# Causal maxima in tiles of 32 tokens by four heads, instead of 128 tokens of one head

## The chip, the cores and the metric

The kernel runs on one core of a Trainium2 chip. The metric is the device time of one execution in microseconds. Before the change it is 818.26 us, the median of 3 runs (817.12 to 818.61).

## The reference, cut to what matters

The program is one transformer layer on 8 sequences (batches) of 256 tokens with 256 features: attention, then a mixture of experts. The change is in the attention alone. There are 32 query heads of width 8, and 8 key heads; each key head serves four query heads.

```python
q = (x @ Wq).reshape(b, T, N_HEADS, hd).transpose(0, 2, 1, 3)
k = (x @ Wk).reshape(b, T, N_KV_HEADS, hd).transpose(0, 2, 1, 3)
...
q = _apply_rope(q, cos, sin)
k = _apply_rope(k, cos, sin)
qg = q.reshape(b, N_KV_HEADS, N_GROUPS, T, hd)
scores = jnp.einsum('bkgtd,bksd->bkgts', qg, k) / jnp.sqrt(jnp.asarray(hd, x.dtype))
causal = jnp.tril(jnp.ones((T, T), dtype=bool))
scores = jnp.where(causal[None, None, None, :, :], scores, jnp.asarray(-jnp.inf, x.dtype))
attn = jax.nn.softmax(scores, axis=-1)
ctx = jnp.einsum('bkgts,bksd->bkgtd', attn, v)
```

Here `T` is 256, `hd` is 8, there are 8 key heads and 4 query heads ("groups") to each. A softmax subtracts from each row of scores its maximum over the keys that the row may see, which are those up to its own token.

## The kernel before

**Two passes over the scores.** The attention of a batch computes its scores twice. The first pass (`maxima`, L461) has tokens on the partitions: TensorE makes scores in PSUM, adds a mask of -1e30 above the diagonal with a second matmul, and VectorE takes the maximum over the keys, with its sign turned (L486). The negated maxima are split into a high and a low part (`split_shift`, L494), turned by TensorE so that heads come to the partitions (`shiftT`, L501), and written by DMAs as extra rows 96 to 101 into the tile of queries. The second pass (`weights_of`, L521) has keys on the partitions; its matmul runs over 102 rows, so the maximum is subtracted inside the matmul. ScalarE takes the exponential (L532), GpSimd clears what lies above the diagonal (L534), and `values` (L545) multiplies by the values.

**Operands.** `qAs` holds the queries turned, as [row, (chunk, group), token]: a chunk is three key heads (the last has two) that share the 96 rows, 32 rows for each head. `ksts` holds the keys, [row, key head, token], with zeros in the rows of the other heads, so that one matmul of a query tile of 96 rows against several key heads gives the scores of each head apart. There are three buffers of each, used by batch modulo 3. `queriesT` (L436) turns the queries on TensorE and copies them by ScalarE into `qAs` (L448), one copy for each chunk and each half of the tokens.

**Tiles of the first pass.** A step has 128 tokens of one query head of a group on the partitions, and two or three key heads times all keys up to the end of the 128 tokens as columns. For the first half of the tokens that is 128 keys, for the second half 256. `maxima_of` (L450) cuts this into steps of at most 512 columns, which is one PSUM tile `sc`. Each matmul of scores (L472) is followed by a matmul of the mask (L479), whose stationary operand is a 128x128 identity in bf16 (`ident_b`), and whose moving operand is the 128x128 triangle `mask`, repeated for each key head. For a batch that makes 26 steps, 32 matmuls of scores and 32 of the mask.

**Order.** All engines run an order that is written out: `at(when, step, ...)` puts each step on a timeline in units of batches, and the steps are issued in the order of `when` (L1197). The maxima of batch b start at b - 0.98, one every 0.032; between them lie the exponentials and values of batch b - 1, the projections of batch b + 1, and, from 1.5 on, the matmuls of the shared experts (`shared_gate_up`, `shared_down`), which fill TensorE. [...]The PSUM tiles of scores, of the second pass and of the experts come from one pool of five buffers (`ps_mm`).

**After the attention** come the blocks of routed experts, which TensorE runs one after another from some 545 us on; the change touches nothing there.

Of the kernel before, what the change touches and what calls it, by code (L numbers as in the profile page):

```python
# [10 lines left out]
F32 = mybir.dt.float32  # L11
F32R = mybir.dt.float32r
BF16 = mybir.dt.bfloat16
I32 = mybir.dt.int32
AF = mybir.ActivationFunctionType
ALU = mybir.AluOpType
AX = mybir.AxisListType
PSUM = bass.MemoryType.PSUM

P = 128  # L20
# [4 lines left out]
SHIFT = 96  # L25
# [5 lines left out]
def attn_moe_kernel(  # L31
# [47 lines left out]
    nc = tc.nc  # L79
    B, T, D = x.shape  # L80
# [11 lines left out]
    G = 4  # L92
    NKV = NH // G
    NK = NKV * HD
    NC = NKV // G
    J = 3
    NS = -(-NKV // J)
    KR = SHIFT + 2 * J
    QSCALE = HD**-0.5
    FT = 4  # L100
    NTOK = NT * P
# [11 lines left out]
    small = ctx.enter_context(tc.tile_pool(name="small", bufs=4))  # L113
    shared_pool = ctx.enter_context(tc.tile_pool(name="shared", bufs=1))
    ps_mm = ctx.enter_context(tc.tile_pool(name="ps_mm", bufs=5, space=PSUM))
# [3 lines left out]
    aconst = early.enter_context(tc.tile_pool(name="aconst", bufs=1))  # L119
# [12 lines left out]
    ident = const.tile([P, P], F32, name="ident")  # L132
# [8 lines left out]
    for w, lo, n in ((wq, 0, D), (wk, D, NK), (wv, D + NK, NK)):  # L141
        nc.scalar.dma_start(
            out=wqkv[:, :, lo : lo + n], in_=w.rearrange("(k p) n -> p k n", p=P)
# [3 lines left out]
    for b in range(1, B):  # L147
# [6 lines left out]
    nc.scalar.dma_start(out=wr_sb, in_=wr)  # L154


    mask = aconst.tile([P, P], BF16, name="mask")
    nc.gpsimd.memset(mask, 0.0)
    nc.gpsimd.affine_select(
        out=mask,  # L160
        in_=mask,
        pattern=[[-1, P]],
        compare_op=ALU.is_ge,
        fill=NEG,
        base=0,
        channel_multiplier=1,
    )
    ident_b = aconst.tile([P, P], BF16, name="ident_b")
    nc.vector.tensor_copy(ident_b, ident)
    ident_r = aconst.tile([P, P], F32R, name="ident_r")  # L170
    nc.vector.tensor_copy(ident_r, ident)

# [4 lines left out]
    for sign, base in ((1, 0), (-1, 1)):  # L177
        nc.gpsimd.affine_select(
            out=place1[SHIFT:P],
            in_=place1[SHIFT:P],  # L180
            pattern=[[-2 * sign, J], [0, 1]],
# [5 lines left out]
    qAs, ksts, v_aug = {}, {}, {}  # L187

    def clear_operands(i):
        qAs[i] = aconst.tile([P, NS * G, T], F32R, name=f"qA_{i}")  # L190
        engine = nc.gpsimd if i > 0 else nc.vector
        engine.memset(qAs[i][:, (NS - 1) * G :, :].bitcast(F32), 0.0)
        t = ksts[i] = aconst.tile([P, NKV, T], F32R, name=f"kst_{i}")
        engine.memset(t[0:SHIFT].bitcast(F32), 0.0)

# [103 lines left out]
    def at(when, step, *args):  # L299
        timeline.append((when, len(timeline), step, args))  # L300
# [100 lines left out]
    def heads_in(c):  # L401
        return min(J, NKV - c * J)
# [33 lines left out]
    def queriesT(b, tt, c):  # L436
        qs = held["qs", b, tt][1]
        n = heads_in(c) * HB
        pt = ps_tp.tile([P, G, P], F32, tag="tp", name=f"pqT{b}_{tt}_{c}")
        for g in range(G):  # L440
            nc.tensor.matmul(
                pt[0:n, g, :],
                lhsT=qs[:, c * G + g, 0:n],
                rhs=ident_r,
                start=True,
                stop=True,
            )
        nc.scalar.copy(qAs[b % 3][0:n, ts(c, G), ts(tt, P)], pt[0:n])  # L448

    def maxima_of(b, tt):  # L450

        width = (tt + 1) * P
        for c in range(NS):
            per = min(512 // width, heads_in(c))
            for k0 in range(0, heads_in(c), per):
                nk = min(per, heads_in(c) - k0)
                ng = 512 // (nk * width)
                for g0 in range(0, G, ng):
                    yield c, c * J + k0, nk, g0, ng

    def maxima(b, tt, c, k0, nk, g0, ng):  # L461

        qA, kst = qAs[b % 3], ksts[b % 3]
        if ("nmx", b, tt) not in held:
            held["nmx", b, tt] = small.tile(
                [P, NKV, G], F32, tag="nmx", name=f"nmx{b}_{tt}", bufs=2
            )
        nmx = held["nmx", b, tt]
        width = (tt + 1) * P
        sc = ps_mm.tile([P, ng, nk, width], F32, tag="mm", name="sc")  # L470
        for g in range(ng):
            nc.tensor.matmul(  # L472
                sc[:, g, :, :],
                lhsT=qA[0:SHIFT, c * G + g0 + g, ts(tt, P)],
                rhs=kst[0:SHIFT, k0 : k0 + nk, 0:width],
                start=True,
                stop=False,
            )
            nc.tensor.matmul(  # L479
                sc[:, g, :, width - P :],  # L480
                lhsT=ident_b,
                rhs=mask.unsqueeze(1).to_broadcast([P, nk, P]),
                start=False,
                stop=True,
            )
        nc.vector.tensor_reduce(  # L486
            nmx[:, k0 : k0 + nk, g0 : g0 + ng].rearrange("p k g -> p g k"),
            sc,
            AX.X,
            ALU.max,  # L490
            negate=True,
        )

    def split_shift(b, tt):  # L494
        nmx = held.pop(("nmx", b, tt))
        nhl = small.tile([P, NKV, 2, G], F32R, tag="nhl", name=f"nhl{b}_{tt}", bufs=2)
        nc.vector.tensor_copy(nhl[:, :, 1, :], nmx)
        nc.vector.tensor_tensor(nhl[:, :, 0, :], nmx, nhl[:, :, 1, :], ALU.subtract)
        held["nhl", b, tt] = nhl

    def shiftT(b, tt):  # L501
        nhl = held.pop(("nhl", b, tt))
        pm = ps_tp.tile([2 * NH, P], F32, tag="tp", name=f"pm{b}_{tt}")
        nc.tensor.matmul(
            pm,
            lhsT=nhl.rearrange("p k a g -> p (k a g)"),
            rhs=ident_r,
            start=True,
            stop=True,
        )  # L510
        nm = work.tile([2 * NH, P], F32R, tag="nm", name=f"nm{b}_{tt}")
        nc.vector.tensor_copy(nm, pm)
        for c in range(NS):
            n = 2 * heads_in(c)
            lo = c * J * 2 * G
            nc.sync.dma_start(
                out=qAs[b % 3][SHIFT : SHIFT + n, ts(c, G), ts(tt, P)].bitcast(F32),
                in_=nm[lo : lo + n * G, :].bitcast(F32),
            )

    def weights_of(b, kv, s, t):  # L521

        sc = ps_mm.tile([P, G, P], F32, tag="mm", name="scT")
        nc.tensor.matmul(  # L524
            sc,
            lhsT=ksts[b % 3][0:KR, kv, ts(s, P)],
            rhs=qAs[b % 3][0:KR, ts(kv // J, G), ts(t, P)],
            start=True,
            stop=True,
        )  # L530
        e = work.tile([P, G, P], F32, tag="ex", name="ex", bufs=EX)
        nc.scalar.activation(e, sc, AF.Exp, scale=QSCALE)  # L532
        if s == t:
            nc.gpsimd.affine_select(  # L534
                out=e,
                in_=e,
                pattern=[[0, G], [1, P]],
                compare_op=ALU.is_ge,
                fill=0.0,
                base=0,  # L540
                channel_multiplier=-1,
            )
        held["ex", b, kv, s, t] = e
# [437 lines left out]
    def turning(xg, b):  # L981


        n = xg.shape[1]
        xgT = ffn.tile([P, KC, n * P], F32, tag=f"xgT{n}", name=f"xgT{b}")
        of = xg.rearrange("p t (k d) -> p k t d", k=KC)
        to = xgT.rearrange("p k (t q) -> p k t q", q=P)

        def step(i):
            for j in range(P // SQ):  # L990
                nc.vector.transpose(  # L991
                    to[ts(j, SQ), :, :, ts(i, SQ)], of[ts(i, SQ), :, :, ts(j, SQ)]
                )

        return xgT, [partial(step, i) for i in range(P // SQ)]
# [66 lines left out]
    for i, a in enumerate((-2.2, -0.93, 0.03)):  # L1062
        at(a, clear_operands, i)
        at((-1.7, a, a)[i], set_ones, i)
        at((-1.97, -0.96, 0.02)[i], clear_values, i)
# [13 lines left out]
    for b in range(B):  # L1079
# [14 lines left out]
        when = b - 0.98  # L1094
        for tt in range(TT):
            for m in maxima_of(b, tt):
                at(when, maxima, b, tt, *m)
                when += 0.032
            at(when + 0.001, split_shift, b, tt)
            at(when + 0.07, shiftT, b, tt)  # L1100
        last = b == B - 1
        parts_of = [(c, t) for c in range(NC) for t in range(TT)]
        when, unit = b, 0.98 / (NC * 3 * G)
        if b == 0:
            parts_of.sort(key=lambda part: part[1])
            when, unit = -0.4, 0.04
        for c, t in parts_of:
            if b == 0 and t > 0:
                when = max(when, 0)
            for s in range(t + 1):  # L1110
                for j in range(G):
                    at(when, weights_of, b, c * G + j, s, t)
                    when += unit
                at(when + 0.05, values, b, c, s, t)
            a = when + (0.1 if last else 0.12)
            at(a, softmaxed, b, c, t)
            if c == NC - 1:
                at(a + 0.05, contextT, b, t)
                at(a + 0.09, projected, b, t)
# [84 lines left out]
    for b in range(NFULL):  # L1204
# [12 lines left out]
        xg, now, steps = held.pop(("xg", b + 1)), xgT, ()  # L1217
        if b + 1 < NFULL:
            xgT, steps = turning(xg, b + 1)
# [122 lines left out]
```

## Time and profile before

| What | Value |
|---|---|
| median of 3 runs | 818.26 us |
| the profiled execution: its own time | 817.86 us |
| the profiled execution: span from first to last instruction | 815.8 us |
| mean granted TensorE clock | 0.97 |
| ScalarE busy | 251.3 us (31%) |
| GpSimd busy | 344.0 us (42%) |
| exponential of the second pass, L532, on ScalarE | 192 times 597 ns |
| copy of the queries, L448, on ScalarE | 48 times, 576 to 580 ns |
| clearing above the diagonal, L534, on GpSimd | 128 times 639 ns |
| matmul of the second pass, L524 | 192 times, 512 columns |
| DMA of the maxima into `qAs`, L514 | 32 of 12 KB and 16 of 8 KB |

The profile names engines PE (TensorE matmuls), PEld (TensorE loads of the stationary operand, which may run beside a matmul), DVE (VectorE), ACT (ScalarE), POOL (GpSimd) and SP. Matmuls are pipelined, so the duration of one is longer than the distance from its start to the start of the next; in a stream it is the distance of the starts that says what a matmul costs.

### The profile page before, as it was taken

The page shows a single profiled execution, that of the slowest core. Times are in us where ns is not written, and L with a number is a line of the kernel's source. Part 1 is how long each engine was busy: PE and PEld are TensorE (multiplying, and loading weights), DVE is VectorE, ACT ScalarE, POOL GpSimd, SP SyncE. Part 2 cuts the span into 40 slices and gives each one's busy share as a digit, 9 for nine tenths or more (in the row PEclk, how much of TensorE's full clock was granted, in tenths as well). Part 3 has the DMA queues.
Part 4 walks back from the last instruction along what each step waited for, and adds up shares of the span by engine and source line. Part 5 has one row for each costly group of instructions (what it writes and reads, how often), then busy time and mean ns, then how long its engine had stood idle before and what let it go on. Part 6 is the DMA issues. An engine that isn't in the chain of part 4 may idle for free. (4 is left out here: it accounts for less than half of the span.)

```text
span 815.8 us, 11856 instructions
## 1 busy us (share of the span) xinstructions
PE 761.7 (93%) x3977; PEld 579.3 (71%) x3977; DVE 492.2 (60%) x1412; ACT 251.3 (31%) x552; POOL 344.0 (42%) x620
## 2 busy tenths in 40 slices
PE   5989899999999999999999998799999999999992
PEld 3544467767776776776766657688888888888991
DVE  5756577667668568568666635547655555742226
ACT  2455344334334334333333431121111111111214
POOL 4567456426436436436324441416223434343323
PEclk8799899999999999999999998899999999999997
DMA  5033300000000000000000002365465665758544
GB/s 155 3 88 90 89 16 16 8 22 15 7 23 14 2 29 14 3 29 14 2 29 2 14 14 90 139 226 169 129 206 168 192 218 157 233 149 271 170 81 155
DMA packets 31011, 70.42 MB, mean 86 GB/s; under 512 B 8560, under 2 KB 25456, under 8 KB 28256
## 3 DMA queue, kind: packets, MB, share of 16 engines
q1 hardware_dynamic: 19504, 54.23, 19.2%
q0 software_dynamic: 8128, 9.77, 6.4%
q10 hardware_dynamic: 3312, 5.60, 2.4%
q8 instruction: 34, 0.56, 0.3%
q14 instruction: 33, 0.27, 0.1%
HBM read 55.16 MB, written 11.80 MB: 82 GB/s over the span
## 5 line engine op out<-in xcount | busy, mean ns | idle before, releaser
L780 PE MATMUL gu<-xgT,w 128*128 128x256 f32 (+1 forms) x840 | 163.9, 354 | 1.0 <-ACT xgT L978 0.7
L780 PEld LDWEIGHTS gu<-xgT,w 128*128 128x128 f32 x840 | 144.5, 190 | 18.1 <-ACT xgT L978 1.0
L532 ACT ACTIVATE ex<-scT 128x512 f32<-128x512 f32 x192 | 113.6, 597 | 137.4 <-PE scT L524 124.9
L780 PE MATMUL gu<-x2T,ws_sb 128*128 128x256 f32 x640 | 152.9, 385 | 0.1
L486 DVE TENSOR_REDUCE nmx<-sc 128x2 f32<-128x512 f32 (+2 forms) x208 | 129.3, 643 | 26.4 <-PE sc L479 26.1
L780 PEld LDWEIGHTS gu<-x2T,ws_sb 128*128 128x128 f32 x640 | 119.8, 193 | 21.3 <-ACT ex L532 3.8
L534 POOL TENSOR_SCALAR_AFFINE_SELECT ex<-ex 128x512 f32<-128x512 f32 x128 | 81.0, 639 | 114.3 <-ACT ex L532 114.1
L1014 POOL DMA_INDIRECT sums<-yb,of x37 | 58.5, 1582 | 109.2 <-DVE yb L1013 71.1
L472 PE MATMUL sc<-kst,qA 96*128 96x512 f32 (+2 forms) x256 | 101.3, 426 | 0.8 <-issue 0.5
L524 PE MATMUL scT<-qA,kst 102*128 102x512 f32 x192 | 97.5, 516 | 1.8 <-DMA qA<-nm 1.8
L1003 ACT ACTIVATE sg<-gu 128x256 f32<-128x256 f32 (+1 forms) x105 | 37.6, 358 | 191.1 <-PE gu L780 154.2
L991 DVE STREAM_TRANSPOSE xgT<-xg 32x128 f32<-32x128 f32 x240 | 72.6, 302 | 29.4 <-DMA xg<-rows,of 20.6
L793 PE MATMUL po<-w,act 128*128 128x256 f32 x370 | 83.1, 379 | 0.0
L793 PE MATMUL po<-ws_sb,sact 128*128 128x256 f32 x320 | 74.7, 391 | 4.6 <-DVE sact L816 4.6
L793 PEld LDWEIGHTS po<-w,act 128*128 128x128 f32 x370 | 69.8, 190 | 9.3
L793 PEld LDWEIGHTS po<-ws_sb,sact 128*128 128x128 f32 x320 | 61.6, 196 | 18.3 <-DVE sact L816 5.0
L479 PE MATMUL sc<-mask,ident_b 128*128 128x256 bf16 (+2 forms) x256 | 74.3, 293 | 0.0
L1004 DVE TENSOR_TENSOR act<-sg,gu 128x256 f32<-128x256 f32 (+1 forms) x105 | 38.8, 388 | 56.8 <-ACT sg L1003 56.2
L815 DVE SCALAR_TENSOR_TENSOR th<-th,gu 128x256 f32<-128x256 f32 x70 | 29.4, 419 | 65.8 <-ACT th L814 65.8
L932 POOL DMA_INDIRECT xg<-rows,of x37 | 35.9, 970 | 63.0 <-DMA of<-slots 47.4
L472 PEld LDWEIGHTS sc<-kst,qA 96*128 96x128 f32 x256 | 51.4, 201 | 13.6 <-issue 3.9
L552 PE MATMUL av<-ex,v_aug 128*32 128x512 f32 x384 | 58.3, 605 | 1.3 <-POOL ex L534 1.3
(171 smaller groups left out, 847.8 us busy)
## 6 DMA issues: line engine op xcount, KB each, us to landing
w<-in_routed SPq DMA_DIRECT2D x21, 1920.0 KB
ws_sb<-in_shared ACTq DMA_DIRECT2D x8, 480.0 KB
xs<-in_x SPq DMA_DIRECT2D x8, 256.0 KB
rows<-x2n SPq DMA_DIRECT2D x8, 256.0 KB
acc<-sums SPq DMA_DIRECT2D x4, 512.0 KB
sums<-ya SPq DMA_DIRECT2D x14, 128.0 KB
kst<-kA SPq DMA_DIRECT2D x16, 96.0 KB
out<-acc SPq DMA_DIRECT2D x6, 256.0 KB
```

Source lines behind the costliest of these rows:

```text
L472: nc.tensor.matmul(sc[:, g, :, :], lhsT=qA[0:SHIFT, c * G + g0 + g, ts(tt, P)], rhs=kst[0:SHIFT, k0 : k0 + nk, 0:width], start=True, stop= ...
L479: nc.tensor.matmul(sc[:, g, :, width - P :], lhsT=ident_b, rhs=mask.unsqueeze(1).to_broadcast([P, nk, P]), start=False, stop=True,)
L486: nc.vector.tensor_reduce(nmx[:, k0 : k0 + nk, g0 : g0 + ng].rearrange("p k g -> p g k"), sc, AX.X, ALU.max, negate=True,)
L524: nc.tensor.matmul(sc, lhsT=ksts[b % 3][0:KR, kv, ts(s, P)], rhs=qAs[b % 3][0:KR, ts(kv // J, G), ts(t, P)], start=True, stop=True,)
L532: nc.scalar.activation(e, sc, AF.Exp, scale=QSCALE)
L534: nc.gpsimd.affine_select(out=e, in_=e, pattern=[[0, G], [1, P]], compare_op=ALU.is_ge, fill=0.0, base=0, channel_multiplier=-1,)
L552: nc.tensor.matmul(av[32 * j : 32 * j + 32, :], lhsT=v_aug[b % 3 * TT + s][:, c * G + j, :], rhs=e.rearrange("p g t -> p (g t)"), start=(s ...
L780: nc.tensor.matmul(gu[:, half, :], lhsT=m[:, k, ts(i, P)], rhs=xT[:, k, :], start=(k == 0), stop=(k == KC - 1),)
L793: nc.tensor.matmul(po, lhsT=act[:, k, ts(t, P)], rhs=d[:, k, :], start=(k == 0), stop=(k == ic - 1),)
L991: nc.vector.transpose(to[ts(j, SQ), :, :, ts(i, SQ)], of[ts(i, SQ), :, :, ts(j, SQ)])
L1004: nc.vector.tensor_tensor(act[:, i, :], sg, gu[:, 1, :], ALU.mult)
L1014: put = nc.gpsimd.indirect_dma_start(out=sums, out_offset=bass.IndirectOffsetOnAxis(ap=of[:, t, 1:2], axis=0), in_=y, in_offset=None, comp ...
```

## The change

The first pass is tiled in another way. A tile has 32 tokens of the four query heads of a group on the 128 partitions, and its keys end where these 32 tokens end: 32, 64, ... 256 keys for the eight tiles of a batch. The triangle of the mask is 32 columns wide and 32 rows deep, and the stationary operand that puts it on the partitions, `token_of`, is a 32x128 bf16 matrix: the 32x32 identity four times. `qAs` gets the layout [row, chunk, tile of 32 tokens, (group, token)], so the copy in `queriesT` writes runs of 32, the exponential reads its scores in another order than it writes them, and the DMAs of `shiftT` write 2 KB to each partition in one run instead of four of 512 B. The small tiles `nmx` and `nhl` have the tile's number where they had the group. One step takes all key heads that fit into 512 columns, of more than one chunk if need be, and there is one pair of matmuls to each chunk that it touches. That makes 21 steps for a batch, and again 32 matmuls of scores and 32 of the mask. The steps are 0.04 apart instead of 0.032.

```diff
+    QB = P // G
+    TQ = P // QB
...
-    mask = aconst.tile([P, P], BF16, name="mask")
+    mask = aconst.tile([QB, QB], BF16, name="mask")
...
-        pattern=[[-1, P]],
+        pattern=[[-1, QB]],
...
-    ident_b = aconst.tile([P, P], BF16, name="ident_b")
-    nc.vector.tensor_copy(ident_b, ident)
+    token_of = aconst.tile([QB, P], BF16, name="token_of")
+    nc.vector.tensor_copy(
+        token_of.rearrange("p (g q) -> p g q", g=G),
+        ident[0:QB, 0:QB].unsqueeze(1).to_broadcast([QB, G, QB]),
+    )
...
-        qAs[i] = aconst.tile([P, NS * G, T], F32R, name=f"qA_{i}")
+        qAs[i] = aconst.tile([P, NS, T // QB, G * QB], F32R, name=f"qA_{i}")
...
-        nc.scalar.copy(qAs[b % 3][0:n, ts(c, G), ts(tt, P)], pt[0:n])
+        to = qAs[b % 3][0:n, c, ts(tt, TQ), :].rearrange("p i (g q) -> p g i q", g=G)
+        nc.scalar.copy(to, pt[0:n].rearrange("p g (i q) -> p g i q", i=TQ))
 
     def maxima_of(b, tt):
 
-        width = (tt + 1) * P
-        for c in range(NS):
-            per = min(512 // width, heads_in(c))
-            for k0 in range(0, heads_in(c), per):
-                nk = min(per, heads_in(c) - k0)
-                ng = 512 // (nk * width)
-                for g0 in range(0, G, ng):
-                    yield c, c * J + k0, nk, g0, ng
-
-    def maxima(b, tt, c, k0, nk, g0, ng):
+        for i in range(TQ):
+            width = (tt * TQ + i + 1) * QB
+            steps = -(-NKV // (512 // width))
+            per = -(-NKV // steps)
+            for k0 in range(0, NKV, per):
+                yield i, k0, min(per, NKV - k0)
+
+    def maxima(b, tt, i, k0, nk):
...
-        width = (tt + 1) * P
-        sc = ps_mm.tile([P, ng, nk, width], F32, tag="mm", name="sc")
-        for g in range(ng):
+        width = (tt * TQ + i + 1) * QB
+        sc = ps_mm.tile([P, nk, width], F32, tag="mm", name="sc")
+        for c in range(k0 // J, -(-(k0 + nk) // J)):
+            k, z = max(k0, c * J), min(k0 + nk, c * J + J)
+            part = sc[:, k - k0 : z - k0, :]
             nc.tensor.matmul(
-                sc[:, g, :, :],
-                lhsT=qA[0:SHIFT, c * G + g0 + g, ts(tt, P)],
-                rhs=kst[0:SHIFT, k0 : k0 + nk, 0:width],
+                part,
+                lhsT=qA[0:SHIFT, c, tt * TQ + i, :],
+                rhs=kst[0:SHIFT, k:z, 0:width],
                 start=True,
                 stop=False,
             )
             nc.tensor.matmul(
-                sc[:, g, :, width - P :],
-                lhsT=ident_b,
-                rhs=mask.unsqueeze(1).to_broadcast([P, nk, P]),
+                part[:, :, width - QB :],
+                lhsT=token_of,
+                rhs=mask.unsqueeze(1).to_broadcast([QB, z - k, QB]),
                 start=False,
                 stop=True,
             )
-        nc.vector.tensor_reduce(
-            nmx[:, k0 : k0 + nk, g0 : g0 + ng].rearrange("p k g -> p g k"),
-            sc,
-            AX.X,
-            ALU.max,
-            negate=True,
-        )
+        nc.vector.tensor_reduce(nmx[:, k0 : k0 + nk, i], sc, AX.X, ALU.max, negate=True)
...
             nc.sync.dma_start(
-                out=qAs[b % 3][SHIFT : SHIFT + n, ts(c, G), ts(tt, P)].bitcast(F32),
-                in_=nm[lo : lo + n * G, :].bitcast(F32),
+                out=qAs[b % 3][SHIFT : SHIFT + n, c, ts(tt, TQ), :].bitcast(F32),
+                in_=nm[lo : lo + n * TQ, :].bitcast(F32),
             )
...
-        sc = ps_mm.tile([P, G, P], F32, tag="mm", name="scT")
+        sc = ps_mm.tile([P, TQ, G * QB], F32, tag="mm", name="scT")
...
-            rhs=qAs[b % 3][0:KR, ts(kv // J, G), ts(t, P)],
+            rhs=qAs[b % 3][0:KR, kv // J, ts(t, TQ), :],
...
-        nc.scalar.activation(e, sc, AF.Exp, scale=QSCALE)
+        nc.scalar.activation(
+            e.rearrange("p g (i q) -> p g i q", i=TQ),
+            sc.rearrange("p i (g q) -> p g i q", g=G),
+            AF.Exp,
+            scale=QSCALE,
+        )
...
-                when += 0.032
+                when += 0.04
```

## The prediction

> **What bounds the kernel now.** I read the page first, its busy shares and its 40 slices, and then a table of stretches (stretch and its length, then busy us and instructions of PE, PEld, DVE, ACT, POOL, then the clock).
>
> ```profile
> PE 761.7 (93%) x3977; PEld 579.3 (71%) x3977; DVE 492.2 (60%) x1412; ACT 251.3 (31%) x552; POOL 344.0 (42%) x620
> ...
> PEclk8799899999999999999999998899999999999997
> ```
>
> ```profile
> 20.00:35.00 15.00, 13.99 (x64) 8.61 (x63) 9.46 (x21) 7.97 (x16) 9.10 (x22) 0.69 0.01 3
> 35.00:54.00 19.00, 15.07 (x82) 8.03 (x81) 12.29 (x28) 9.02 (x19) 12.72 (x31) 0.98 0.26 70
> 54.00:90.00 36.00, 33.05 (x180) 19.10 (x179) 23.11 (x56) 18.69 (x38) 20.13 (x60) 0.96 0.36 101
> 90.00:125.00 35.00, 32.42 (x173) 20.54 (x173) 24.42 (x73) 15.70 (x32) 18.74 (x40) 0.90 0.08 25
> 125.00:187.00 62.00, 60.30 (x340) 43.00 (x339) 41.68 (x119) 23.35 (x50) 28.99 (x62) 1.00 0.05 15
> 187.00:249.00 62.00, 60.82 (x346) 43.77 (x344) 42.95 (x121) 22.87 (x50) 29.05 (x63) 1.00 0.06 15
> ```
>
> From 125 to 442 us, where most maxima lie, TensorE is busy for 309.9 of 317 us at full clock (the five stretches of that table), so it idles 2%, while VectorE, the next, is busy for about 70%. There what TensorE saves is saved in the span: its order is fixed, and the others have room to come sooner. From 35 to 125 us (the rest of batch 0, batch 1 and part of batch 2) it idles 9.5 of 90 us; there a part of a saving can turn into waits.
>
> So the change is worth what it saves on TensorE, and a stream is priced by distances of starts, not by durations. These are rows of the order of time (start, duration):
>
> ```profile
> 30.72 0.36 PE L472 MATMUL sc<-kst,qA 96*128 96x256 f32 x1
> 30.93 0.28 PE L479 MATMUL sc<-mask,ident_b 128*128 128x256 bf16 x1
> 30.96 0.36 PE L472 MATMUL sc<-kst,qA 96*128 96x256 f32 x1
> 31.17 0.28 PE L479 MATMUL sc<-mask,ident_b 128*128 128x256 bf16 x1
> ...
> 35.55 0.23 PE L479 MATMUL sc<-mask,ident_b 128*128 128x128 bf16 x1
> 35.60 0.36 PE L472 MATMUL sc<-kst,qA 96*128 96x256 f32 x1
> 35.80 0.23 PE L479 MATMUL sc<-mask,ident_b 128*128 128x128 bf16 x1
> ...
> 83.08 0.28 PE L479 MATMUL sc<-mask,ident_b 128*128 128x256 bf16 x1
> 83.12 0.48 PE L472 MATMUL sc<-kst,qA 96*128 96x512 f32 x1
> 83.44 0.28 PE L479 MATMUL sc<-mask,ident_b 128*128 128x256 bf16 x1
> ...
> 173.11 1.06 PE L665 MATMUL pl<-wr_sb,x2T 128*128 128x8 f32 x8
> 174.03 0.48 PE L524 MATMUL scT<-qA,kst 102*128 102x512 f32 x1
> ```
>
> A pair of 256 columns of scores and 256 of mask takes 0.24 us from mask to mask (30.93 to 31.17); with a mask of half the columns it takes 0.25 (35.55 to 35.80). So 128 columns less of mask save nothing: the mask hides the next load of a stationary operand, and that sets the time. The eight router matmuls show the floor: 8 columns each, and still 0.92/8 = 0.115 us from start to start. With 512 columns of scores the pair takes 0.36 us (83.08 to 83.44), so 256 columns of scores cost 0.115, or 0.43 ns a column. A pair whose mask is short thus costs 0.43 ns a column of scores and 0.137 us (0.247 - 256 x 0.43 ns) that is fixed.
>
> **The change part by part: TensorE.** The number of pairs stays, 32 for a batch. Before: 12 pairs of 512 columns and 256 of mask at 0.36; 8 of 384 and 384 at an estimated 0.35 (by the column prices: 0.165 for each of the two, plus what is exposed); 12 of 256 columns at 0.247. Sum 4.32 + 2.80 + 2.96 = 10.1 us a batch, 80.7 in all. After: the widths 32 to 256 times eight key heads are 9,216 columns of scores instead of 12,288, and every mask has 32 to 96 columns, so all masks lie under the 0.115 us floor. 9,216 x 0.43 ns + 32 x 0.137 = 3.96 + 4.38 = 8.34 us, 66.8 in all. **TensorE saves 1.74 us a batch, 13.9 in all.**
>
> Here a rule speaks for more. The Trainium skill, "TensorE: Matmul & The Clock Gate", section "Step-by-step: what each phase is for", says that a stream of matmuls costs purely its columns. Scores and mask together lose 9,216 of 20,480 columns a batch, so by the rule 3.96 us a batch and 31.7 in all would go. The row of the router at 0.115 us for 8 columns denies it for short matmuls, and I take the row.
>
> **What the trace does not show: the load of token_of.** It is 32 rows by 128 columns of bf16. The nearest row is ident_b's, 128 by 128:
>
> ```profile
> L472 PEld LDWEIGHTS sc<-kst,qA 96*128 96x128 f32 x256 | 51.4, 201 | 13.6 <-issue 3.9 <-DVE nmx L486 1.7 <-ACT ex L532 1.2
> ...
> L479 PEld LDWEIGHTS <-ident_b 128*128 128x128 bf16 x256 | 25.5, 99 | 41.4 <-issue 35.2
> ```
>
> It takes 99 ns, half of a 4-byte load (201), and it waits for "issue" most times, that is, it is not loaded ahead. So what it is longer by stands on the path. The same page, section "Weight-path perf modes — Fast Weight Load (FWL) and DoubleRow", says that the fast load comes on with 128 columns of weights of a type that is not fp32, and puts no condition on rows; by it token_of costs 99 ns too. Upper end: 201 ns, 0.102 x 256 = 26 us more. Lower end: nothing gained, since fewer rows make no load shorter in the rows for 96 and 102 of 128 (198 to 201 ns). I take 99. A matmul of 32 rows next to one of 96 is not in the trace either; the pair 128 and 96 holds about 0.02 us that neither columns nor load explain (0.247 less 0.11 and 0.115), so up to once more of that, 5 us, stays in the range.
>
> **VectorE.** Reductions fall from 26 to 21 a batch and from 12,288 to 9,216 elements a partition. 512 elements take 684 ns and 384 take 551, so 1.04 ns an element and 0.15 us each: 129.3 us become 8 x (9,216 x 1.04 ns + 21 x 0.15) = 102. The 27 us lie beside TensorE (DVE busy 43 of 62 us), so I count nothing; were an output of 32 elements dearer, the 19 us idle in a stretch of 62 cover it.
>
> **Edits counted at nothing.** The exponential reads PSUM in runs of 32: no row shows it. Lower end none, since the elements are the same; upper end a doubling, 24 x 0.6 = 14 us a batch on ACT, which idles 39 of 62. The matmul of values after it would only be hurt where TensorE has no filler, before 110 us. The six query copies a batch write in runs of 32, under the same cover (at worst 3.5 us). The shift DMAs keep number and bytes; SP has nothing late behind them. They stand by the timeline at (21 x 0.04 + 0.07) instead of (26 x 0.032 + 0.07), 0.008 batch or 0.5 us later for the second half, which is read first 0.23 batch later; for the first half 0.08 batch earlier. The first tile needs the copies of all three chunks where it needed one: the fifth copy in ACT's order ends at 20.8 us, when the first scores start anyway. Smaller mask set-up on POOL and VectorE is hidden by the load of x, for which VectorE waits until 4.15 us. The reductions still wait on PE, and ps_mm's five buffers come free sooner.
>
> **Sum.** Batches 2 to 7: 6 x 1.74 = 10.4. Batch 0's first tiles run at a clock of about 0.7, so its saving is larger, some 2.9 (8 pairs of 0.66 us in the order of time become narrower ones); with batch 1 that is 4.6, of which I take half, as the stretches up to 125 us have waits of their own: 2.3. Together 12.7, less 0.2 for the start. Against the profiled execution (817.86 us, span 815.8) that gives 805.4; the median of the runs is 0.4 above that execution, so **805.5 us**. The likeliest case's own range is 799 to 812: 5 us less for the change of rows, 6 us more if the start keeps its share and VectorE's relief takes away waits (TensorE's 7 us idle from 125 to 442).
>
> **Rivals.**
> - Columns decide, not loads: 817.9 - 31.7 = 786, up to 792 if the start keeps half. For it: the streams of experts do go by columns. Against: the rows above. 6%.
> - The load of token_of is slow (201 ns) and not hidden: 805 + 26 = 831. It decides against the change from 50 ns more a pair on (12.5/256), so slower by any reading beyond 150 ns. For it: no load with 32 rows is in the trace, and the load is exposed. Against: the rule, and equal loads with 96 and 102 rows. 10%.
> - TensorE's saving becomes waits: 815 to 818. POOL's and VectorE's chain through projections and splits would have to set the pace. For it: waits before 125 us. Against: 29 and 43 of 62 us busy later. 8%.
>
> The likeliest case has 76%. The measurement can tell 0.2%, 1.6 us. Faster: 76 + 6 + half of the third = 86%; same 4%; slower 10%. Range 793 to 815: it leaves out the slow load and the pure columns, and takes in the start of the third.
>
> **What would show it.** In the changed profile, pairs of short scores stand about 0.17 to 0.25 us from mask to mask; LDWEIGHTS of token_of at 99 ns; L486's successor near 102 us for 168 reductions; PE busy less by about 13 us, its waits in 125 to 430 us near 2%. Loads of 200 ns, or pairs of 0.3 us with 200 columns, make the prediction wrong on one side, pairs under 0.1 us on the other.

## The result, and the profile after

The changed kernel takes 873.19 us, median of 4 runs (867.03 to 875.02), against 817.69 us before. The ratio is 1.0665, with a 95% interval of 1.061 to 1.0719. The forecast was 805.5 us: wrong by 68 us, and in sign. The profiled execution took 872.46 us with a span of 870.7 us. Its page, first the busy shares and the clock of the 40 slices, then three of the groups:

```profile
PE 819.1 (94%) x3977; PEld 609.2 (70%) x3977; DVE 470.4 (54%) x1372; ACT 251.0 (29%) x552; POOL 345.7 (40%) x620
...
PEclk8557957999999999999999999889999999999997
...
L533 ACT ACTIVATE ex<-scT 128x512 f32<-128x512 f32 x192 | 113.7, 597 | 159.6 <-PE scT L525 148.1
...
L493 DVE TENSOR_REDUCE nmx<-sc 128x2 f32<-128x384 f32 (+5 forms) x168 | 101.9, 612 | 63.6 <-PE sc L486 63.3
...
L486 PEld LDWEIGHTS <-token_of 32*128 32x128 bf16 x256 | 23.5, 92 | 56.1 <-issue 48.1
```

VectorE fell to 102 us as computed, the exponential takes the same 597 ns, and the load of `token_of` is fast (92 ns). Yet TensorE, with fewer columns to run, is busy for 57 us more. The granted clock is lower, too: 0.93 in the mean instead of 0.97, and near half in slices 2, 3 and 6. The same stretches as before:

```profile
35.00:54.00 19.00, 19.00 (x61) 10.90 (x64) 8.22 (x15) 6.35 (x14) 8.91 (x24) 0.50 0.17 43
54.00:90.00 36.00, 34.10 (x157) 19.57 (x150) 14.85 (x38) 17.54 (x34) 15.66 (x43) 0.77 0.20 57
90.00:125.00 35.00, 31.25 (x114) 16.82 (x113) 16.51 (x42) 9.99 (x20) 18.01 (x47) 0.71 0.26 75
...
187.00:249.00 62.00, 59.95 (x312) 41.90 (x310) 36.58 (x107) 20.52 (x45) 25.62 (x54) 0.97 0.05 15
```

From 187 to 249 us it is about as busy as before (59.95 us, then 60.82), but gets 312 matmuls done instead of 346, a tenth less at a clock that is 3% lower. So the matmuls themselves became dearer, and the order of time, now with the loads (PEld), shows which:

```profile
242.93 0.09 PEld L486 LDWEIGHTS <-token_of 32*128 32x128 bf16 x1
242.94 0.21 PE L486 MATMUL sc<-mask,token_of 32*128 32x96 bf16 x1
243.08 0.19 PEld L479 LDWEIGHTS sc<-kst,qA 96*128 96x128 f32 x1
243.08 0.35 PE L479 MATMUL sc<-kst,qA 96*128 96x192 f32 x1
243.36 0.09 PEld L486 LDWEIGHTS <-token_of 32*128 32x128 bf16 x1
243.37 0.21 PE L486 MATMUL sc<-mask,token_of 32*128 32x96 bf16 x1
```

A pair of 192 columns takes 0.43 us from mask to mask; the forecast price was 0.22. In the profile before, the load of the next queries starts with the mask and lies under it. Between the prediction's rows at 35.55 (mask) and 35.60 (scores) stands:

```profile
35.56 0.20 PEld L472 LDWEIGHTS sc<-kst,qA 96*128 96x128 f32 x1
```

Here it starts at 243.08, 0.14 us after the mask, together with the matmul that needs it: nothing is loaded ahead any more, and every column of the mask counts. Pairs in a row, from 190 to 500 us, lie within 6 ns of 0.305 us + 0.42 ns for each column of scores and of mask: 0.372 with 64 and 96 columns, 0.387 with 96 and 96, 0.431 with 256 and 32. By the forecast it was 0.137 us + 0.43 ns for the columns of scores alone.

### The profile page after: what moved, and what is told of

Read it like the earlier page. It is cut to its first block, busy times and chain, and to the rows that moved or that the text cites. A ratio compares the mean times of both kernels' runs of the same rounds, so it can differ in the third digit from the quotient of the medians.

```text
span 870.7 us, 11817 instructions
## 1 busy us (share of the span) xinstructions
PE 819.1 (94%) x3977; PEld 609.2 (70%) x3977; DVE 470.4 (54%) x1372; ACT 251.0 (29%) x552; POOL 345.7 (40%) x620
## 4 chain that ended last, share of the span: by engine, by line
PE 83%; DVE 9%; POOL 3%; issue 2%; ACT 2%; DMA 1%; ACTq 0%; POOLq 0%; DVEq 0%
PE gu L786 34%; PE po L799 18%; PE scT L525 6%; PE sc L479 6%; PE av L558 5%; PE sc L486 3%; PE pqT L446 2%; PE pq L352 2%; PE py L605 2%; PE pav L578 2%; PE pl L671 1%; DVE nmx L493 1%; DVE st L284 1%; POOL r L290 1%; POOL ex L540 1%
## 5 line engine op out<-in xcount | busy, mean ns | idle before, releaser
L786 PE MATMUL gu<-x2T,ws_sb 128*128 128x256 f32 x640 | 159.8, 398 | 0.0
L786 PEld LDWEIGHTS gu<-x2T,ws_sb 128*128 128x128 f32 x640 | 123.1, 198 | 23.9 <-DVE nmx L493 2.5
L493 DVE TENSOR_REDUCE nmx<-sc 128x2 f32<-128x384 f32 (+5 forms) x168 | 101.9, 612 | 63.6 <-PE sc L486 63.3
L525 PE MATMUL scT<-qA,kst 102*128 102x512 f32 x192 | 103.0, 545 | 1.9 <-DMA qA<-nm 1.9
L479 PE MATMUL sc<-kst,qA 96*128 96x192 f32 (+11 forms) x256 | 104.3, 407 | 0.0
L799 PE MATMUL po<-ws_sb,sact 128*128 128x256 f32 x320 | 78.9, 406 | 4.6 <-DVE sact L822 4.6
L799 PEld LDWEIGHTS po<-ws_sb,sact 128*128 128x128 f32 x320 | 64.1, 204 | 19.6 <-DVE sact L822 5.0
L479 PEld LDWEIGHTS sc<-kst,qA 96*128 96x128 f32 x256 | 54.6, 213 | 22.6 <-issue 9.3
L486 PEld LDWEIGHTS <-token_of 32*128 32x128 bf16 x256 | 23.5, 92 | 56.1 <-issue 48.1
L558 PE MATMUL av<-ex,v_aug 128*32 128x512 f32 x384 | 59.4, 637 | 0.9 <-POOL ex L540 0.9
```

The costliest lines, as they stand in the source:

```text
L479: nc.tensor.matmul(part, lhsT=qA[0:SHIFT, c, tt * TQ + i, :], rhs=kst[0:SHIFT, k:z, 0:width], start=True, stop=False,)
L486: nc.tensor.matmul(part[:, :, width - QB :], lhsT=token_of, rhs=mask.unsqueeze(1).to_broadcast([QB, z - k, QB]), start=False, stop=True,)
L493: nc.vector.tensor_reduce(nmx[:, k0 : k0 + nk, i], sc, AX.X, ALU.max, negate=True)
L525: nc.tensor.matmul(sc, lhsT=ksts[b % 3][0:KR, kv, ts(s, P)], rhs=qAs[b % 3][0:KR, kv // J, ts(t, TQ), :], start=True, stop=True,)
L558: nc.tensor.matmul(av[32 * j : 32 * j + 32, :], lhsT=v_aug[b % 3 * TT + s][:, c * G + j, :], rhs=e.rearrange("p g t -> p (g t)"), start=(s ...
L786: nc.tensor.matmul(gu[:, half, :], lhsT=m[:, k, ts(i, P)], rhs=xT[:, k, :], start=(k == 0), stop=(k == KC - 1),)
```

## What the experiments told apart

Three theories stood at first. **A**: the 32 rows of the mask's matmul, next to 96 of the scores, make TensorE drain (let one matmul run out before the next begins) and load nothing ahead. **B**: masks of 32 to 96 columns are too short to cover a load. **C**: less work in the array lowers the granted clock.

**128 rows.** The mask and its stationary operand are filled up with rows of zeros; all else of the change stays.

```diff
-    mask = aconst.tile([QB, QB], BF16, name="mask")
+    mask = aconst.tile([128, QB], BF16, name="mask")
...
-    token_of = aconst.tile([QB, P], BF16, name="token_of")
+    token_of = aconst.tile([128, P], BF16, name="token_of")
+    nc.vector.memset(token_of, 0.0)
...
-                rhs=mask.unsqueeze(1).to_broadcast([QB, z - k, QB]),
+                rhs=mask.unsqueeze(1).to_broadcast([128, z - k, QB]),
```

> The changed kernel, with the mask and its stationary operand filled up with rows of zeros to 128 rows; columns, tiles and layouts stay. Theory A (rows: after a matmul of 32 rows TensorE drains and loads nothing ahead, which costs 0.18 us a pair): pairs go back to 0.137 us + 0.42 ns a column of scores, the granted clock back to about 0.97, time 800 to 812. Theory B (columns: a mask of 32 to 96 columns is too short to hide the next load, whatever its rows): pairs stay at 0.37 to 0.44 us, time 865 to 875. Theory C (less array work by itself makes the clock fall): pairs short, but clock still about 0.92, time 825 to 850.

It took 825.81 us, ratio 1.0093 (1.0059 to 1.0127): 47 of the 55 us are gone. A pair of 192 columns in its order of time:

```profile
244.23 0.19 PE L487 MATMUL sc<-mask,token_of 128*128 128x32 bf16 x1
244.23 0.20 PEld L480 LDWEIGHTS sc<-kst,qA 96*128 96x128 f32 x1
244.27 0.34 PE L480 MATMUL sc<-kst,qA 96*128 96x192 f32 x1
244.44 0.10 PEld L487 LDWEIGHTS <-token_of 128*128 128x128 bf16 x1
244.44 0.19 PE L487 MATMUL sc<-mask,token_of 128*128 128x32 bf16 x1
```

The load starts with the mask again, and the pair takes 0.21 us. All sizes are within 8 ns of the price of the prediction: 0.157 us with 64 columns of scores, 0.172 with 96, 0.246 with 256. Against the same pairs of the changed kernel that is 0.18 to 0.22 us less: 0.11 on the way to the mask, 0.07 to 0.10 on the way back. Theory B falls; A holds for the pairs. But the time is some 20 us above what A alone should give. It lies in the range of theory C, and the clock, 0.953, lies between what A (0.97) and C (0.92) expected, so C is not out yet.

**96 rows and 64 rows**, as above with other numbers.

> As the one with 128 rows, but filled up to 96 rows, the number that the matmul of scores has. Theory A, if what counts is that both have the same rows or both more than 64: as with 128 rows, 800 to 812, perhaps a few us less as scores and mask then have equal rows. If only 128 rows will do: 850 to 875. Theory B: 865 to 875.

> The changed kernel with the mask and its operand filled up to 64 rows. If a matmul of at most 64 rows is a different state of the array from one of 96 to 128 rows, and a change between the two states drains it: pairs at 0.37 to 0.44 us as with 32 rows, 865 to 880. If only 32 rows do that: pairs at 0.16 to 0.25, 820 to 830.

With 96 rows 825.2 us, ratio 1.0094 (1.0058 to 1.013), and the same pairs as with 128 (within 3 ns); the time is again above the range of A. With 64 rows 875.97 us, ratio 1.0722 (1.0692 to 1.0753), and pairs as with 32:

```profile
240.55 0.21 PE L487 MATMUL sc<-mask,token_of 64*128 64x96 bf16 x1
240.69 0.35 PE L480 MATMUL sc<-kst,qA 96*128 96x192 f32 x1
240.98 0.21 PE L487 MATMUL sc<-mask,token_of 64*128 64x96 bf16 x1
```

So equal rows are not needed (128 by 96 is well). A change between up to 64 rows and 96 or more is what costs. The Trainium skill has two statements that fit. "TensorEngine Tiling (Array Packing)", section "Key Properties", says: "Changing tiling mode (not just tile) drains the TensorE". Its section "When to Use Tiling" assigns contractions of 64 rows and of 32 to modes of their own. It does not say that a plain matmul of so few rows runs in such a mode by itself; the border that the runs found, between 64 and 96 rows, agrees with it. No price stands there. The runs put it at 0.18 to 0.22 us for the way to the mask and back; how much of that is the drain and how much the load that no longer runs ahead, they do not tell apart.

**The kernel before, with 32 rows.** Its masks keep 128 to 384 columns; the mask of 96 of each 128 tokens is left out.

```diff
-                lhsT=ident_b,
-                rhs=mask.unsqueeze(1).to_broadcast([P, nk, P]),
+                lhsT=ident_b[0:32],
+                rhs=mask[0:32].unsqueeze(1).to_broadcast([32, nk, P]),
```

> The kernel before, with the mask's matmul cut to its first 32 rows (the mask of the other 96 tokens of a tile is left out); columns stay 128 to 384. Theory A: a pair of 256 columns of scores and 128 of mask goes from 0.246 to 0.305 us + 0.42 ns x 384 = 0.47 us, 0.2 us more on each of 256 pairs, and the clock falls: 865 to 890. Theory B (columns): no change, 815 to 820.

It took 884.77 us, ratio 1.0811 (1.0753 to 1.0868). Its pairs of 256 columns of scores and 128 of mask take 0.471 us instead of 0.246, as expected (0.47), and those with 256 of mask 0.53:

```profile
270.34 0.28 PE L479 MATMUL sc<-mask,ident_b 32*128 32x256 bf16 x1
270.55 0.38 PE L472 MATMUL sc<-kst,qA 96*128 96x256 f32 x1
270.87 0.28 PE L479 MATMUL sc<-mask,ident_b 32*128 32x256 bf16 x1
```

The rows alone thus make the old kernel slow too, with its long masks. Its mean clock fell to 0.93 although all columns stayed. So the clock falls without fewer columns; whether the drains lower it or the fewer rows at work, no run tells apart.

**One mask for a step.** From the version with 128 rows on: the scores of all chunks first (only the first opens the bank), then one mask over all of them, 21 masks a batch instead of 32.

```diff
-                start=True,
+                start=(k == k0),
...
-            nc.tensor.matmul(
-                part[:, :, width - QB :],
+        nc.tensor.matmul(
+            sc[:, :, width - QB :],
```

> The version with 128 rows, and one mask matmul for a step in place of one for each chunk: 21 instead of 32 a batch, with 32 to 256 columns. Theory A: each of the 88 masks that go saves about 0.12 us: 10 us less than the version with 128 rows, 790 to 802. Theory B: masks of up to 256 columns hide the load again, so better than 870 by 30 us or more, about 830 to 840.

819.02 us, ratio 1.0005 (0.9986 to 1.0024): 7 us less than with 128 rows, where A expected 10, but again some 20 above the level expected.

**Where the rest stayed.** Two stretches of the same length, 187 to 374 us, first of the kernel before, then of the version with 128 rows (busy us of PE, PEld, DVE, ACT, POOL):

```profile
187.00:374.00 187.00, 183.33 (x1036) 131.41 (x1034) 130.07 (x365) 69.58 (x149) 87.60 (x187) 1.00 0.05 15
```

```profile
187.00:374.00 187.00, 177.71 (x1035) 129.45 (x1034) 120.75 (x349) 67.74 (x147) 87.69 (x186) 1.00 0.05 15
```

TensorE does as many matmuls at the same clock in 5.6 us less, 1.9 us a batch where 1.74 were forecast, and idles for it. What it waits for there, in the version with 128 rows (us, times, longest):

```profile
PE pm L506 <- DVE kA L431: 3.0, 3, 1.2
PE pav L579 <- DVE rb L372: 3.0, 3, 1.0
PE pqT L447 <- DVE kA L431: 0.8, 2, 0.4
PE pqT L447 <- DVE cx L586: 0.7, 3, 0.2
...
```

Before, only the wait of `pav` is there, 3.0 us. `pm`, `pqT` and `pav` do not read `kA`, `rb` or `cx`; they need the PSUM buffer that these read from. All are tiles of the pool of two for turnings (`ps_tp`), and VectorE gives a buffer back late. The start of the first router matmul (`pl`) of a batch measures the way to it. The table has it in us, from one profiled execution of each version (those below the third line are told of further down), with the time that the clock stood at half before that of batch 0:

| version | batch 0 | half clock until then | batch 1 | batch 5 | batches 1 to 5, each |
|---|---|---|---|---|---|
| before | 111.2 | 24 | 173.1 | 419.6 | 61.6 |
| changed | 136.8 | 83 | 207.2 | 473.7 | 66.6 |
| 128 rows | 117.0 | 42 | 183.5 | 429.4 | 61.5 |
| 128 rows, old place | 113.5 | 34 | 175.4 | 419.3 | 61.0 |
| 128 rows, copies on ScalarE | 113.1 | 37 | 174.8 | 416.9 | 60.5 |
| 128 rows, third buffer | 111.1 | 31 | 172.3 | 415.0 | 60.7 |
| 128 rows, filled | 114.3 | 34 | 176.6 | 422.6 | 61.5 |
| all | 112.3 | 31 | 173.6 | 416.2 | 60.6 |
| all, copies on ScalarE | 112.2 | 31 | 173.7 | 411.1 | 59.4 |
| all, third buffer | 110.1 | 27 | 171.0 | 407.5 | 59.1 |
| all, copies and third buffer | 108.7 | 24 | 170.3 | 406.9 | 59.2 |

The version with 128 rows loses 10.4 us up to batch 1 and gains next to nothing after it. Two further theories came from this. **D**: the step that turns the maxima of a first half comes earlier now, between the turnings of keys and queries of the next batch, and meets their buffers. **D2**: two buffers are too few in any order.

**The old place in the order.**

```diff
-            at(when + 0.07, shiftT, b, tt)
+            at(when + (0.07 if tt else 0.15), shiftT, b, tt)
```

> The version with 128 rows, with the turning of the first half's maxima 0.08 of a batch later, where it stood before the change; nothing else. Theory D (place in the order: 21 steps instead of 26, six of them in the first half, put that step between the turnings of keys and queries of the next batch, which share two PSUM buffers with it, and TensorE waits there 2 us a batch): these waits go, 62.3 us a batch become about 60.3, time 811 to 818. If they only move elsewhere: 823 to 828.

> 128 rows, one mask for a step, the turning at its old place, masks not filled. Theory D: 808 to 812. Otherwise as the one with one mask, 817 to 821.

On the version with 128 rows 818.46 us, ratio 1.0025 (0.9995 to 1.0056), just above what D expected. In 187 to 374 us the waits of `pm` are gone, but `pqT` now waits 2.6 us for `kA`: most waits moved. By the table a batch became 0.5 us shorter, not the 2 us of theory D. Of the 10.1 us that its profile gained up to batch 5, 8.1 came before batch 1, where the clock stood at half for 34 us instead of 51. With one mask a step 815.23 us, ratio 0.9954 (0.9925 to 0.9983), between the two expectations.

**Who empties a buffer**: the copies of the keys on ScalarE, which idles more than half of a batch.

```diff
-        copied = copier(b - 1)
+        copied = nc.scalar.copy
```

> The version with 128 rows, with the copies of the turned keys (kA) on ScalarE in all batches, not on VectorE from the third on. If VectorE's queue of reductions in front of that copy is what holds a ps_tp buffer: the waits of pm and pqT for kA go, some 1 us a batch, time 817 to 822. If the lack of buffers counts and not who empties them: 823 to 828.

815.55 us, ratio 0.9983 (0.9957 to 1.0009): 10 us less, more than expected. The waits for `kA` are gone; `pav` for `rb` stays. A batch takes 60.5 us instead of 61.5, as expected of these waits; most of the rest again came before batch 1.

**A third buffer**, taken from the pool of scores.

```diff
-    ps_mm = ctx.enter_context(tc.tile_pool(name="ps_mm", bufs=5, space=PSUM))
-    ps_tp = ctx.enter_context(tc.tile_pool(name="ps_tp", bufs=2, space=PSUM))
+    ps_mm = ctx.enter_context(tc.tile_pool(name="ps_mm", bufs=4, space=PSUM))
+    ps_tp = ctx.enter_context(tc.tile_pool(name="ps_tp", bufs=3, space=PSUM))
```

> The version with 128 rows, with three PSUM buffers for the turnings (ps_tp) and four for the scores (ps_mm), instead of two and five. Theory D2 (what TensorE saves is lost in waits for one of the two ps_tp buffers, which ACT, and above all VectorE, give back late): waits before pm, pqT, pav and px go, 62 us a batch become 59.5 to 60.5, time 808 to 815. Rival E (TensorE idles because another engine's chain sets 62 us a batch): waits show elsewhere, before sc, scT or av, time 822 to 830.

> The kernel before, with three ps_tp and four ps_mm buffers. There the waits for ps_tp are 1 us a batch (pav for rb alone): by D2 811 to 816, so that the tiles of 32 tokens keep a lead; if four ps_mm buffers are too few, 818 to 825.

With 128 rows 818.45 us, ratio 1.0005 (0.9975 to 1.0035), 7 us less, between what D2 and its rival E expected. A batch takes 60.7 us; the waits of `pav` are gone, and some waits are now for the four buffers of scores. The kernel before becomes slower by it, 823.75 us, ratio 1.0069 (1.0034 to 1.0105). In 187 to 374 us its scores wait for their four buffers (2.7 us of `sc` and 1.5 us of `scT`), a little more than `pav` had waited. But its batches take 61.9 us, only 0.3 more, and it reaches batch 5 at 416.8 us, 2.8 us sooner than with two buffers. From there to the end it loses 7.3 us, more than half of it in the routed experts, which take their PSUM tiles from the same pool. These two waits of 504 to 816 us are not in the profile before:

```profile
PE gu L780 <- DVE act L1004: 2.0, 4, 0.7
PE gu L780 <- DVE yb L1013: 1.9, 3, 1.1
```

The versions with 128 rows pay this as well: from batch 5 to the end 394.6 us with two buffers, 399.2 with three. So a time of the whole program shows less than what a third buffer brings to the attention.

**Filled masks.** Up to 256 columns of zeros in front of the triangle:

```diff
...
+            wide = min(width, 256 // (z - k) // QB * QB)
             nc.tensor.matmul(
-                part[:, :, width - QB :],
+                part[:, :, width - wide :],
                 lhsT=token_of,
-                rhs=mask.unsqueeze(1).to_broadcast([128, z - k, QB]),
+                rhs=mask[:, T - wide :].unsqueeze(1).to_broadcast([128, z - k, wide]),
```

> The version with 128 rows, with the mask widened by columns of zeros up to 256 columns a matmul, which lie under the next load. Theory C (the granted clock follows the work in the array; the columns that the change took from the masks cost no time, but kept the clock up): the pairs keep their times, half clock up to 200 us falls from 51 us to 25 to 35, time 815 to 820. Otherwise: clock as with 128 rows, time 824 to 830, or more where 256 columns are too many to hide.

> 128 rows, copies of the keys on ScalarE, and masks filled with columns of zeros up to 256. Theory C (clock follows the columns): half clock before the first router matmul falls from the 37.5 us of the version without filling to below 30, time 810 to 813. Otherwise 814 to 818.

The columns are free, as the first profile had it: a pair of 256 columns takes 0.246 us with 256 columns of mask as with 64. On the version with 128 rows 820.77 us, ratio 1.0061 (1.0028 to 1.0094), 5 us less, with intervals that overlap. On the one with copies on ScalarE 811.55 us, ratio 0.9936 (0.9921 to 0.9951), 4 us less, without overlap. Theory C has some support in this. The mean clock, as the median over all runs of a version, rose with the filling both times, from 0.953 to 0.966 and from 0.962 to 0.969, while that of the kernel before lay between 0.970 and 0.974. Half clock up to 200 us fell from 51 to 34 us in the first profile, as C expected, and its time is just above C's range; the second has C's time (810 to 813), but 34 us at half clock where C expected less than 30. The time per batch at full clock did not change (61.5 us in the first). Against C stands that the unfilled version with the turning at its old place has 34 us as well. So columns of zeros went with a higher clock; that they alone set it is not shown.

**All together**: 128 rows, one mask a step, filled, old place; then with the copies, the third buffer, or both.

> All together: 128 rows, one mask for a step, its columns filled up to 256, the turning of the first half's maxima at its old place. Theories C and D both: 819 less 8 less 8, 800 to 806. D alone: 808 to 812. Neither: 817 to 821.

> 128 rows, one mask a step, filled, turning at its old place, copies of the keys on ScalarE, two ps_tp buffers. If who empties the buffers counts: as much below 814 as the copies alone brought to the version with 128 rows, 10 us: 803 to 807. If its waits had gone with the turning's place already: 811 to 815.

> The version with all of it (128 rows, one mask for a step, filled columns, turning at its old place), with three ps_tp and four ps_mm buffers. Theory D2: 2 us a batch less than 814, 800 to 808. Rival E: 812 to 820.

> As the one with all and the copies on ScalarE, and three ps_tp and four ps_mm buffers. With the waits for ps_tp gone already by the third buffer the copies add little: 803 to 808; if both shorten waits: 798 to 803.

| version | median us | ratio (95% interval) |
|---|---|---|
| all | 814.02 | 0.996 (0.9936 to 0.9984) |
| all, copies on ScalarE | 809.2 | 0.9918 (0.9889 to 0.9947) |
| all, third buffer | 806.26 | 0.9857 (0.9828 to 0.9886) |
| all, copies and third buffer | 807.59 | 0.9879 (0.9861 to 0.9896) |

The first lies between what D alone and neither theory expected, the second between its two expectations, the third where D2 had it, the fourth where it was expected if the two do not add up. They do not: a batch takes 60.6 us with neither, 59.4 with the copies, 59.1 with the third buffer and 59.2 with both, which speaks for one cause: how long the turnings hold their buffers. With the third buffer the largest waits of 187 to 374 us are short, and none is for a turning:

```profile
PE scT L527 <- ACT ex L535: 1.2, 3, 0.4
PE gu L788 <- ACT ex L535: 0.8, 2, 0.4
PE sc L480 <- ACT ex L535: 0.7, 1, 0.7
PE sc L480 <- DVE nmx L495: 0.6, 2, 0.3
```

A batch takes 59.1 us instead of 61.6 in the kernel before, and the whole 1.4% less. That is the tiles of 32 tokens together with fewer masks and a third buffer; the kernel before got only the third buffer, which made it slower, and was not tried with the copies on ScalarE.

## Why the prediction was wrong, by its steps

**The step that failed first**: "A matmul of 32 rows next to one of 96 is not in the trace either [...] so up to once more of that, 5 us, stays in the range." The cost is 0.18 to 0.22 us a pair, not 0.02. For 256 pairs at 0.2 that is 51 us, and taking it away brought 47: the version with 128 rows waits more, and how much the clock adds (83 us at half before the first router matmul, then 42) is not told apart. The prediction bounded the load of `token_of` from both sides, and the switch of rows only by a residue of a pair without such a switch. Two things spoke against that. The rule of the tiling page, quoted above, was not weighed. And the profile before has a switch, of columns: the values (`av`) use 32 of 128 columns. These are its rows:

```profile
115.34 0.29 PE L479 MATMUL sc<-mask,ident_b 128*128 128x256 bf16 x1
115.56 0.16 PEld L552 LDWEIGHTS av<-ex,v_aug 128*32 128x32 f32 x8
115.56 1.06 PE L552 MATMUL av<-ex,v_aug 128*32 128x512 f32 x8
...
118.18 0.28 PE L479 MATMUL sc<-mask,ident_b 128*128 128x256 bf16 x1
118.18 1.61 PEld L780 LDWEIGHTS gu<-x2T,ws_sb 128*128 128x128 f32 x8
118.30 1.89 PE L780 MATMUL gu<-x2T,ws_sb 128*128 128x256 f32 x8
```

After a mask of 256 columns the experts' matmul starts 0.12 us later and its load with the mask; that of the values starts 0.22 us later and its load only then. That is 0.09 to 0.10 us for the way in. The way out costs the same: in the single records the second four of these eight matmuls start 0.43 us after the first four, but whatever follows them starts after 0.52. Had a switch of rows been priced like this one of columns, it would have been an estimated 0.19 x 256 = 49 us: slower, and near the measured 47. The rival with the slow load had the right sign and the wrong mechanism; the load took 92 ns.

**The step that failed next**: "There what TensorE saves is saved in the span: its order is fixed, and the others have room to come sooner." Shares of busy time do not tell whether a result comes in time. In the version with 128 rows TensorE saved 1.9 us a batch and the batch stayed at 61.5 us, since three of its turnings waited for one of two buffers; in the versions with everything else, freeing the buffers sooner or adding a third took 1.3 to 1.5 us off a batch. That was the third rival, given 8%. It named chains through POOL and VectorE; it was two PSUM buffers and VectorE's place in line. The change itself moved one turning next to two others, which the prediction priced by when its result is read, not by the buffer that it takes.

**The start.** Half of 4.6 us was to be saved; the version with 128 rows lost 10.4 us up to the router matmul of batch 1 instead. Of the 256 pairs 117 lie before it, so by the forecast 5 us of its 12.5 were to be gained up to there: 15 us are missing. The clock stood at half for 51 us of that stretch, against 24. Work that takes all of TensorE's time loses half of each such us, an estimated 14 us for the 27 more, so the clock alone is nearly enough. What sets it there is left open. After batch 1 the forecast had 7.6 us to gain, and 2.2 were gained. Together that is the 20 us that were left when the rows were filled up.

**A slip in the sum**: 805.4 us and the 0.4 between execution and median make 805.8, not 805.5. It decides nothing.

**What was right.** The price of a pair without a switch: 0.137 us and 0.43 ns a column, within 8 ns. TensorE's saving of 1.74 us a batch (1.9), where the switch is gone. The load at 99 ns or a little less. VectorE's 102 us. The exponential (597 ns before and after) and the query copies (582 ns in the median, before and after). No run took the other edits of layout back, so that they cost nothing is likely but not shown.

## What to carry to other kernels

A contraction of 32 or 64 rows between matmuls of 96 cost about 0.2 us each time here; rows of zeros up to 96 or 128 took that away at no cost that the pairs show, and were worth 47 us. Before counting on a saving on the busiest engine, look at what each of its instructions needs besides data: a buffer of a small pool that a late engine gives back eats the saving, and a step that moves next to others of its pool makes it worse. When an edit makes a state that the trace does not show, look for the nearest switch of state that it does show and price a rival by it, not by a residue of rows without one.

## What the runs showed of the hardware

- A mask's columns cost nothing while they lie under the next load of 128 columns: with 256 columns of scores, masks of 32 to 256 columns gave the same pair, 0.246 us.
- With a mask of 32 or 64 rows a pair took 0.18 to 0.22 us more than with 96 or 128, and the next load started with its own matmul instead of with the mask.
- A matmul of 32 columns of 128 (`av`) after one of 128 columns started 0.09 to 0.10 us late, and so did what followed it.
- The granted clock fell with masks of 32 rows, not only with fewer columns: the kernel before with 32 rows has all its columns and a mean clock of 0.93 instead of 0.97. It can be at half while TensorE's records show no idle time: from 35 to 54 us of the changed kernel it was 0.50 with TensorE busy for all 19.00 us.
- Columns of zeros that cost no time in the pairs went with a higher mean clock: 0.966 instead of 0.953, and 0.969 instead of 0.962.
